# A graph layer on one core: the last 24 edge blocks in half steps, paced dense work, and a last layer with nodes as rows

## The chip, the cores and the metric

The kernel runs on one core of one Trainium2 chip. The metric is device time in microseconds (us) of one execution; "before" is the kernel as it stood, "after" the kernel with the change described below. The time of an execution is a little longer than the span of its trace, which runs from the first to the last instruction that the profiler recorded.

The engines are named as in the profile: PE is TensorE (matrix products; PEld its weight loads), DVE is VectorE (elementwise work), ACT is ScalarE (activations), POOL is GpSimd (here it only issues gathers), SP is SyncE (here it only issues the other transfers). A name with a q, as SPq, is an engine's sequencer.

## The reference

There are 8192 nodes with 256 channels and 131072 edges with 64 channels, sorted by destination. One graph layer with attention is computed, added to its input, and normalized:

```python
ea  = edge_attr @ w_e + b_e
msg = relu(x[src] + ea)
agg = segment_sum(msg, dst)                          # per destination node
h_local = bn(relu((x + agg) @ w1 + b1) @ w2 + b2 + x)
# attention inside groups of 32 nodes, 4 heads of 64 channels
h_attn  = bn(softmax(q k^T / 8) v @ out_w.T + out_b + x)
out = h_local + h_attn
out = bn3(out + relu(out @ m_w1 + m_b1) @ m_w2 + m_b2)
return layernorm(x + out)                            # over the 256 channels
```

Each `bn` is a multiplication and an addition by constants of the channel. All data are float32.

## The kernel before, in words

**Edges.** The edges are cut into NB = 128 blocks of 1024. For a block, `gather` (L152) has POOL issue eight indirect transfers, each of 128 rows of `x` (of `xb`, which is x + b_e, from block 20 on) into the tile `xs`, of which there are four. `load_edges` and `edge_transpose` bring the edge attributes and turn them. `edge_products` (L195) has PE multiply them by `w_e` into two double banks of PSUM, one for each pair of the block's four groups of 256 edges (tag `pe`, two buffers). `edge_messages` (L219) adds the gathered rows on DVE (L229) and takes the relu on ACT (L233). `edge_sums` (L255) multiplies the messages by one-hot matrices (L250, 16 PE instructions into the one bank with tag `pw`) and ACT copies the result to `ws` (L263). `edge_place` (L270) multiplies `ws` by a second one-hot matrix, which puts the rows at their nodes (L278, four PE instructions), and DVE adds that to the transposed node features `xT` (L287).

**Nodes.** The nodes are cut into 16 chunks of 512. `attention_front` and `attention_back` leave the attention's part in the tile `hA`, with channels as rows and nodes as columns. `dense` (L533) does the rest for a part of a chunk once all edge blocks that can reach its nodes are placed: layer w1 (ACT relu, L553), layer w2 (DVE adds it to `hA`, L556), layer m_w1 (ACT relu, L562), ACT's scaled copy `zT` of `hA` (L567), layer m_w2 (DVE adds it, scaled by s3, to `zT`, L574), PE transposes of `zT` back to nodes as rows (L583), the addition of x (L589), the normalization (L591 to L601), and the transfer out on SP's queue (L606). A layer's product for 128 nodes and 128 output channels is four PE instructions of 128 columns; it goes into one of three banks with tag `at`. The 128 nodes of the last quarter of chunk 15 need edge block 127, those of its third quarter block 126, of its second block 124, of its first block 122.

**Order.** PE's instructions are issued in the order in which the code emits them. DVE's and ACT's order is that of the code for the first 26 blocks; after that a scheduler sets it, and `tc.issue_after(i)` makes what follows stand behind instruction `i` on that engine. From block TAIL = 104 on, a plan written out by hand sets the order: a clock `t` is moved forward by an assumed cost for each step; rows of block i are assumed to have come at `came[i]` = 7.9 + 10.035 (i + 1); edge steps are emitted when they are due (`times`), and between them `Work.step` (L682) emits steps of four streams of node work in turns, at most one step of a stream each 0.5 us beyond its cost. `newest` holds the last `ws` copy and the last `xT` addition; the messages of a block are put behind both (L838 to L841). In the plan before, a block's products, messages and sums are emitted for the whole block at once, and block 127's messages are cut into pieces of one group and, for the last group, of 128 edges.

The last parts run in two streams, DENSE and DENSE2, with tiles of their own: chunk 14 in two halves, chunk 15 in four quarters. When the plan has placed block 127, `work.finish` emits what is left of both streams in turns.

Of the kernel before, what the change touches and what calls it, by code (L numbers as in the profile page):

```python
# [41 lines left out]
TAIL = 104  # L42
AGG_ROWS = N + 2 * P
# [29 lines left out]
def gnn_kernel(ctx: ExitStack, tc: tile.TileContext, x, src, dst, edge_attr, w, out):  # L73
# [62 lines left out]
    c3 = const.tile([P, KC], FP, name="c3")  # L136

# [55 lines left out]
    pe_of, msg_of, oh_of, newest = {}, {}, {}, {}  # L193
# [25 lines left out]
    def edge_messages(b):  # L219

        xs = xs_of.pop(b)
        msg = msg_of[b] = epool.tile([P, NH, TJ, C], FP, name="msg", tag="msg", bufs=3)
        n = 2 if b < NB - 1 else 1
        for h in range(0, NH, 2):
# [29 lines left out]

    def edge_sums(blocks):  # L255

        n = len(blocks)
        pw = pps.tile([P, 2, C], FP, name="pw", tag="pw", bufs=1)
        for i, b in enumerate(blocks):
            turns = [(h, j) for j in range(TJ) for h in range(NH)]  # L260
            group_sums(pw, i, b, sorted(turns) if b == NB - 1 else turns)
# [271 lines left out]
    def dense(n0, st, pool, bank, a=0, z=CH, own=("h1", "m1", "zT", "y", "")):  # L533
# [18 lines left out]
        for o in range(KC):  # L552
            nc.scalar.activation(h1[:, o, :], layer(w1, KC, o, tT), AF.Relu, bias=v_("b1", o))  # L553
            yield 1.7 * part
        for o in range(KC):
            nc.vector.scalar_tensor_tensor(  # L556
                hA[:, o, :], layer(w2, KC, o, h1), s1[:, o : o + 1], hA[:, o, :], op0=ALU.mult, op1=ALU.add
            )
            yield 1.7 * part
        m1 = pool.tile([P, 2 * KC, w], FP, name="m1", tag=own[1])  # L560
        for o in range(2 * KC):
            nc.scalar.activation(m1[:, o, :], layer(mw1, KC, o, hA), AF.Relu, bias=v_("m_b1", o))  # L562
            yield 1.7 * part
# [9 lines left out]
        for o in range(KC):  # L573
            nc.vector.scalar_tensor_tensor(  # L574
                zT[:, o, :], layer(mw2, 2 * KC, o, m1), s3[:, o : o + 1], zT[:, o, :], op0=ALU.mult, op1=ALU.add
            )
            yield 3.4 * part
# [26 lines left out]
        for wt, ts in groups:  # L604
# [3 lines left out]
            )  # L608
        yield 0.0
# [33 lines left out]
    class Work:  # L643
# [5 lines left out]
        def __init__(self, n):  # L649
            self.streams = [[] for _ in range(n)]  # L650
            self.rest, self.turn, self.owed = [0] * n, 0, 0.0
            self.at, self.placed_at = [0.0] * n, 0.0

# [28 lines left out]
        def step(self, t, until):  # L682

            n = len(self.streams)
            for i in [k % n for k in range(self.turn, self.turn + n)]:
                while self.streams[i] and self.streams[i][0][0]() and t >= self.at[i]:
# [6 lines left out]
                    elif d > 0:  # L693
                        t += d
                        self.at[i], self.turn = t + 0.5, (i + 1) % n
# [14 lines left out]
    with tc.manual_schedule(engines={PE}):  # L710
# [9 lines left out]
        for c in range(NCH):  # L720
# [11 lines left out]
            if c < NCH - 2:  # L732
                work.add(DENSE, summed(c), dense(c * CH, st, npool, bank))
        for i, c, a, z in (
            (DENSE2, NCH - 2, 0, CH // 2), (DENSE, NCH - 2, CH // 2, CH), (DENSE2, NCH - 1, 0, P),
            (DENSE, NCH - 1, P, 2 * P), (DENSE2, NCH - 1, 2 * P, 3 * P), (DENSE, NCH - 1, 3 * P, CH),
        ):
            d = dense(c * CH, chunk[c], npool, bank, a, z, *([OTHER] if i == DENSE2 else []))
# [10 lines left out]
        while b < TAIL:  # L749
# [11 lines left out]

            if b:
# [29 lines left out]
        t, p, m, s, l = came[b - 2] + 20, b, b, b - 2, b - 2  # L792
# [180 lines left out]
```

## Time and profile before

| | before |
|---|---|
| time, median of 3 runs | 1315.99 us (1314.24 to 1318.11) |
| profiled execution: time, span | 1315.85 us, 1314.1 us |
| PE, DVE, ACT, POOL busy | 91%, 61%, 45%, 74% of the span |
| mean granted TensorE clock | 0.96 |
| read from HBM, written to it | 222.06 MB, 16.78 MB |

In the page's groups a row gives the line, the engine, the operation, what it writes and reads, the count, then busy us and the mean ns of one, then the idle time just before them and what ended it. A row of the timeline gives the start and the duration in us, the engine, the line and the tiles of instructions merged into one row, and in brackets the idle time before it and what ended that. A row of the stretches gives, for a window in us, the length and mean of it, each engine's busy time with its count of instructions, the granted TensorE clock (1.00 is full), the share of DMA time and the GB/s. The profiler's matmul durations contain a pipeline latency, so the pace of matmuls is read from their starts.

### The profile page before, as it was taken

Reading aid. Unit: us, or ns where it says so; the run is one execution under the profiler, and the core shown is the slowest. Engines: PE = TensorE matmul, PEld = TensorE weight load, DVE = VectorE, ACT = ScalarE, POOL = GpSimd, SP = SyncE. Lnnn points to the kernel's source line nnn. Section 1 sums busy time; section 2 is a strip of 40 time slices with the busy share of each in tenths; the row PEclk is TensorE's granted clock in tenths of the full one; section 3 lists DMA queues with packets and bytes.
Section 4 is the critical chain, followed back from the end, with each engine's and each line's share of the span. In section 5 each row is a group of like instructions: output and inputs, shape, how many; then the busy total and the mean of one; then the engine's idle time right before and its main releaser. Section 6 shows DMA issues by size and latency. Waiting matters only on the chain.

```text
span 1314.1 us, 21073 instructions
## 1 busy us (share of the span) xinstructions
PE 1198.9 (91%) x7683; PEld 722.8 (55%) x7683; DVE 803.9 (61%) x1634; ACT 592.0 (45%) x850; POOL 975.3 (74%) x1032
## 2 busy tenths in 40 slices
PE   5987989999999989898997999889898999989986
PEld 3554646556565555555564555545555555555665
DVE  6567665757566565745746574565647558475663
ACT  2524444454545264443544444354454445453443
POOL 7777777777777777777777777777777777777772
PEclk8989999999999989898999999989899999999998
DMA  9999976677666666665767566576566567665741
GB/s 230 280 328 275 280 216 166 175 188 192 169 182 158 171 181 159 188 163 152 195 163 185 153 185 169 154 186 169 169 170 191 149 168 194 162 168 154 193 135 48
DMA packets 148922, 240.35 MB, mean 183 GB/s; under 512 B 27950, under 2 KB 112204, under 8 KB 148044
## 3 DMA queue, kind: packets, MB, share of 16 engines
q0 software_dynamic: 49152, 134.28, 38.6%
q1 hardware_dynamic: 98572, 104.65, 29.4%
q8 instruction: 62, 1.02, 0.3%
q14 instruction: 48, 0.39, 0.1%
q10 hardware_dynamic: 1088, 0.00, 0.0%
HBM read 222.06 MB, written 16.78 MB: 182 GB/s over the span
## 4 chain that ended last, share of the span: by engine, by line
POOL 34%; PE 31%; issue 16%; DMA 9%; DVE 8%; ACT 2%; SPq 0%; DVEq 0%; POOLq 0%; ACTq 0%
POOL xs L157 34%; PE at L546 8%; DMA xs<-xb,srci 6%; PE pe L208 6%; PE at L443 3%; PE pw L250 3%; PE pe L203 2%; PE at L524 2%; DVE msg L229 2%; PE l L278 1%; DVE bd L504 1%; PE at L512 1%; PE at L457 1%; DMA xb<-xp 1%; DVE eaT L190 1%
## 5 line engine op out<-in xcount | busy, mean ns | idle before, releaser
L157 POOL DMA_INDIRECT xs<-xb,srci x864 | 819.1, 948 | 263.2 <-issue 247.7
L233 ACT ACTIVATE msg<-msg 128x1024 f32<-128x1024 f32 (+1 forms) x259 | 270.0, 1046 | 401.4 <-DVE msg L229 397.4
L229 DVE TENSOR_TENSOR msg<-pe,xs 128x1024 f32<-128x1024 f32 (+1 forms) x259 | 306.6, 1207 | 196.5 <-PE pe L208 91.2
L208 PE MATMUL pe<-we,eaT 64*128 64x256 f32 x2048 | 270.3, 401 | 13.5 <-ACT pr L484 9.8
L208 PEld LDWEIGHTS pe<-we,eaT 64*128 64x128 f32 x2048 | 195.4, 194 | 117.9 <-issue 62.8
L157 POOL DMA_INDIRECT xs<-in_x_dram,srci x144 | 138.8, 964 | 43.9 <-issue 40.8
L250 PE MATMUL pw<-msg,oh 128*32 128x256 f32 x2048 | 129.8, 385 | 1.2 <-ACT msg L233 0.8
L546 PE MATMUL at<-hA,mw 128*128 128x512 f32 (+2 forms) x320 | 125.8, 520 | 4.5 <-DVE hA L556 4.3
L443 PE MATMUL at<-xT,inT 128*128 128x512 f32 x256 | 121.8, 602 | 3.2 <-ACT xT L433 3.2
L546 PE MATMUL at<-m,mw 128*128 128x512 f32 (+2 forms) x320 | 119.4, 517 | 0.0
L190 DVE STREAM_TRANSPOSE eaT<-ea 128x512 f32<-128x512 f32 x128 | 90.0, 703 | 22.0 <-PE pe L208 18.6
L250 PEld LDWEIGHTS pw<-msg,oh 128*32 128x32 f32 x2048 | 59.9, 110 | 63.6 <-issue 22.8
L278 PEld LDWEIGHTS l<-oh,ws 128*128 128x128 f32 x512 | 73.7, 195 | 27.3 <-issue 21.4
L278 PE MATMUL l<-oh,ws 128*128 128x160 f32 (+4 forms) x512 | 85.9, 308 | 1.8 <-ACT ws L263 1.7
L546 PEld LDWEIGHTS at<-hA,mw 128*128 128x128 f32 x320 | 55.1, 192 | 53.4 <-issue 41.2
L546 PEld LDWEIGHTS at<-m,mw 128*128 128x128 f32 x320 | 55.7, 192 | 48.0 <-issue 44.8
L443 PEld LDWEIGHTS at<-xT,inT 128*128 128x128 f32 x256 | 46.9, 191 | 57.4 <-issue 47.6
L446 ACT ACTIVATE qk<-at,vec 128x512 f32<-128x512 f32 x64 | 43.8, 685 | 73.7 <-PE at L443 73.6
L546 PE MATMUL at<-xT,w 128*128 128x512 f32 (+2 forms) x160 | 66.3, 551 | 8.8 <-DVE xT L287 8.8
L562 ACT ACTIVATE m<-at,vec 128x512 f32<-128x512 f32 (+2 forms) x80 | 47.9, 599 | 58.5 <-PE at L546 58.0
L546 PE MATMUL at<-h,w 128*128 128x512 f32 (+2 forms) x160 | 65.3, 532 | 9.4 <-ACT oT L519 7.0
L241 DVE TENSOR_TENSOR oh<-iota_n,rel 128x128 f32<-128x128 f32 x256 | 57.6, 279 | 18.2 <-PE pw L250 14.8
(111 smaller groups left out, 1200.7 us busy)
## 6 DMA issues: line engine op xcount, KB each, us to landing
ea<-in_edge_attr_dram SPq DMA_DIRECT2D x512, 128.0 KB
xs<-xb,srci POOLq DMA_INDIRECT x864
xn<-in_x_dram SPq DMA_DIRECT2D x16, 512.0 KB
out_dram<-y SPq DMA_DIRECT2D x14, 512.0 KB
xp<-in_x_dram SPq DMA_DIRECT2D x10, 512.0 KB
xb<-xp SPq DMA_DIRECT2D x10, 512.0 KB
xp<-in_x_dram SPq DMA_DIRECT2D x3, 1024.0 KB
xb<-xp SPq DMA_DIRECT2D x3, 1024.0 KB
```

Of the source, the lines that this page charges most:

```text
L157: nc.gpsimd.indirect_dma_start(out=xs[:, h, j, :], out_offset=None, in_=x if b < NX else xb[:, :], in_offset=bass.IndirectOffsetOnAxis(ap= ...
L190: nc.vector.transpose(eaT, ea[:, QR:].rearrange("p (g d) -> p g d", d=ED)[:, :, :QR])
L208: nc.tensor.matmul(pe[:, i, u, :], eaT[rows, h + u], we[rows, :], start=(b >= NX), stop=True, skip_group_check=True)
L229: nc.vector.tensor_add(msg[:, hs, js].rearrange("p u i c -> p i u c"), pe[:, js, u : u + n, :], xs[:, hs, js].rearrange("p u i c -> p i u c"),
L233: nc.scalar.activation(msg[:, hs, js], msg[:, hs, js], AF.Relu)
L241: nc.vector.tensor_tensor(oh[:, ts], iota_n[:, None, :WN].to_broadcast([P, TB // 2, WN]), rel[:, b, ts, None].to_broadcast([P, TB // 2, WN ...
L250: nc.tensor.matmul(pw[h * WN : (h + 1) * WN, i, :], oh_of[b][:, h * TJ + j, :], msg_of[b][:, h, j, :], start=(j == 0), stop=(j == TJ - 1), ...
L278: nc.tensor.matmul(l2[:, k, at : at + wn], ws[:, i, k * P : (k + 1) * P], oh2[:, i, :wn], start=(i == 0 and k == 0), stop=(i == last), ski ...
L443: nc.tensor.matmul(ps, inT[:, k, o * P : (o + 1) * P], xT[:, k, :], start=(k == 0), stop=(k == KC - 1))
L446: nc.scalar.activation(qk[:, o, :], ps, AF.Identity, bias=v_("in_b", o))
L546: nc.tensor.matmul(ps, wt[:, k, o * P : (o + 1) * P], act[:, k, :], start=(k == 0), stop=(k == nk - 1))
L562: nc.scalar.activation(m1[:, o, :], layer(mw1, KC, o, hA), AF.Relu, bias=v_("m_b1", o))
```

## The change

1. *Halves.* From block 104 on, products, messages and sums are emitted for two groups at a time (`pairs`, `some_sums`). The plan lets the first half's messages stand 2.5 us before the second half's. For block 127 the sums of three groups go first, and those of the last group after its rows. The gather of block i + 2 is emitted with the first half of block i's products. The messages now also stand behind the newest relu of node work on ACT and the newest addition of node work on DVE.
2. *Pacing.* Between `came[115]` and `came[124]` in the plan's clock, node work is given SHARE = 0.42 of the time. The second half of chunk 14 becomes two quarters.
3. *Rows.* `dense_rows` replaces `dense` for the quarters of chunk 15. The first three layers stay. The last one takes `m1` as the stationary and `mw2` as the moving operand, so that its result has nodes as rows; x + c3 (DVE, then a product with the identity), `hA` scaled by s3 (a product with a diagonal matrix) and the layer are summed in one bank, and normalized from there. Transposes, `zT` and its additions are gone for these parts. For the last quarter (`ahead`) the product of x + c3 is emitted before the sums of block 127's last group, and its banks come partly from the tag `pe`.
4. *Set-up.* At block 12 PE makes four transposes of s3 and c3; DVE multiplies `mw2` by s3, copies c3 as a row and makes the diagonal matrices. `dense` then adds with a plain addition instead of one with a scale.

```diff
-            nc.vector.scalar_tensor_tensor(
-                zT[:, o, :], layer(mw2, 2 * KC, o, m1), s3[:, o : o + 1], zT[:, o, :], op0=ALU.mult, op1=ALU.add
-            )
+            newest["dense"] = nc.vector.tensor_add(zT[:, o, :], layer(mw2, 2 * KC, o, m1), zT[:, o, :]).ins
...
+    def dense_rows(n0, st, pool, bank, a, own=("h1", "m1", "zT", "y", ""), ahead=False):
...
+        nc.vector.tensor_add(y, st["xn"][:, a // P, :], c3row)
+
+        def sum_of_x():
+            ps = bank()[:, :C]
+            nc.tensor.matmul(ps, ident, y, start=True, stop=False, skip_group_check=True)
+            return ps
...
+        if ahead:
+            out_ps = sum_of_x()
+            yield 0.45
+        h1 = pool.tile([P, KC, P], FP, name="h1", tag=own[0])
+        for o in range(KC):
+            for _, ps in layer(w1, KC, [o], xT):
+                newest["relu"] = nc.scalar.activation(h1[:, o, :], ps, AF.Relu, bias=v_("b1", o)).ins
+            yield 0.45
+        for o, ps in layer(w2, KC, range(KC), h1):
+            newest["dense"] = nc.vector.scalar_tensor_tensor(
+                hA[:, o, :], ps, s1[:, o : o + 1], hA[:, o, :], op0=ALU.mult, op1=ALU.add
+            ).ins
+        yield 0.9
+        m1 = pool.tile([P, 2 * KC, P], FP, name="m1", tag=own[1])
+        for o0 in range(0, 2 * KC, 2):
+            for o, ps in layer(mw1, KC, range(o0, o0 + 2), hA):
+                newest["relu"] = nc.scalar.activation(m1[:, o, :], ps, AF.Relu, bias=v_("m_b1", o)).ins
+            yield 0.9
+        if not ahead:
+            out_ps = sum_of_x()
+            yield 0.45
+        for k in range(KC):
+            nc.tensor.matmul(
+                out_ps[:, k * P : (k + 1) * P], hA[:, k, :], diag[:, k, :], start=False, stop=False,
+                skip_group_check=True,
+            )
+        yield 0.45
+        for k in range(2 * KC):
+            nc.tensor.matmul(
+                out_ps, m1[:, k, :], mw2[:, k, :], start=False, stop=(k == 2 * KC - 1), skip_group_check=True
+            )
+            if k == KC - 1:
+                yield 0.9
+        nc.vector.bn_stats(st6, out_ps)
+        nc.vector.bn_aggr(mv, st6)
+        nc.scalar.activation(rstd, mv[:, 1:2], AF.Sqrt, bias=eps_t)
+        yield 0.9
+        nc.vector.reciprocal(rstd, rstd)
+        nc.vector.tensor_scalar(y, out_ps, mv[:, 0:1], rstd, ALU.subtract, ALU.mult)
+        nc.sync.dma_start(out[ds(n0 + a, P), :], y)
...
+            if self.paced_from <= t < self.paced_to:
+                self.credit += SHARE * (t - max(self.seen, self.paced_from))
+                self.seen = t
+                if self.credit < -0.02:
+                    return min(until, t - self.credit / SHARE)
...
+            if b == 12:
+                ps = bank()[:, : 2 * C].rearrange("p (i c) -> p i c", i=2)
+                for i, cols in enumerate((s3, c3)):
+                    for k in range(KC):
+                        nc.tensor.transpose(
+                            ps[:, i, k * P : (k + 1) * P], cols[:, k : k + 1].to_broadcast([P, P]), ident
+                        )
+                nc.vector.tensor_mul(mw2, mw2, ps[:, 0, None, :].to_broadcast([P, 2 * KC, C]))
+                nc.vector.tensor_copy(c3row, ps[:, 1, :])
+                for k in range(KC):
+                    nc.vector.tensor_scalar(diag[:, k], ident, s3[:, k : k + 1], None, ALU.mult)
...
+        work.paced_from, work.paced_to = came[115], came[124]
...
-            if l < s:
-                times[0] = summed_at[l] + 1.5
-            elif s < m:
-                times[1] = max(added[s] + 1.2, bank_free)
-                if s == NB - 1:
-                    times[1] = max(came[s] + 2.2, bank_free)
-            if p < NB - 1 and m == p:
-                times[2] = added[p - 1]
-            if m < p:
-                times[3] = came[m]
+            if l < s[0]:
+                times[0] = summed_at[l] + 0.7
+            elif (s[0], s[1] + (s[0] == NB - 1)) < tuple(m):
+                i, k = s
+                times[1] = max(added[i, k] + 1.2, bank_free)
+                if i == NB - 1:
+                    times[1] = max(came[i] + (0.2, 1.0)[k], bank_free)
+            if p[0] < NB and (p[0] - 1, p[1]) < tuple(m):
+                times[2] = added[p[0] - 1, p[1]]
+            if tuple(m) < tuple(p):
+                times[3] = came[m[0]] - 2.5 * (1 - m[1])
...
+                some_sums(i, last if k else range(last.start))
+                t += 0.14 * TJ * (len(last) if k else last.start)
+                if k:
+                    sums = edge_sums([i])
+                    summed_at[i] = t
+                elif i == NB - 1:
+                    next(last_part)
```

More of the change, by code (lines that the diff above doesn't have):

```diff
@@ L253, in group_sums, with some_sums @@
             )
+    def some_sums(b, groups):
+        if b not in pw_of:
+            pw_of[b] = pps.tile([P, 2, C], FP, name="pw", tag="pw", bufs=1)
+        group_sums(pw_of[b], 0, b, [(h, j) for h in groups for j in range(TJ)])
     def edge_sums(blocks):
         n = len(blocks)
[L258 to L261, printed above, removed]
+        pw = pw_of.pop(blocks[0], None)
+        if pw is None:
+            pw = pps.tile([P, 2, C], FP, name="pw", tag="pw", bufs=1)
+            for i, b in enumerate(blocks):
+                group_sums(pw, i, b, [(h, j) for j in range(TJ) for h in range(NH)])
         ws = epool.tile([P, 2, C], FP, name="ws", tag="ws", bufs=2)
```

117 lines of the change are left out of this document (78 added, 39 removed).

## The prediction

> **What bounds the kernel now.** I read the page first, then POOL's rows of the timeline, then the timeline of the last 50 us with all engines, and the granted clock there.
>
> ```profile
> span 1314.1 us, 21073 instructions
> PE 1198.9 (91%) x7683; PEld 722.8 (55%) x7683; DVE 803.9 (61%) x1634; ACT 592.0 (45%) x850; POOL 975.3 (74%) x1032
> ...
> L157 POOL DMA_INDIRECT xs<-xb,srci x864 | 819.1, 948 | 263.2 <-issue 247.7
> ```
>
> ```profile
> 4.31 1.10 POOL L157 DMA_INDIRECT xs<-in_x_dram,srcd  x1 [2.71 <-issue]
> ...
> 1288.01 0.95 POOL L157 DMA_INDIRECT xs<-xb,srci  x1 [0.30 <-issue]
> 1289.26 0.94 POOL L157 DMA_INDIRECT xs<-xb,srci  x1 [0.30 <-issue]
> ```
>
> PE is the busiest engine, but POOL sets the pace: its 74% is a gather of 0.95 us, then 0.30 us of issue, without a wait. 1023 steps of 1.25 us (1289.26 - 1288.01) make 1279 of the 1284.95 us between the first gather and the last. So nothing ahead of 1289.26 moves the end unless it stops a gather. What a change can win is the tail behind it:
>
> ```profile
> 1276.33 1.07 PE L250 MATMUL pw<-msg,oh 128*32 128x256 f32 x16
> ...
> 1279.25 0.94 POOL L157 DMA_INDIRECT xs<-xb,srci  x1 [0.30 <-issue]
> ...
> 1282.08 1.23 DVE L229 TENSOR_TENSOR msg<-pe,xs 128x1024 f32<-128x1024 f32 x1 [1.34 <-DMA xs<-xb,srci]
> ...
> 1283.34 1.06 ACT L233 ACTIVATE msg<-msg 128x1024 f32<-128x1024 f32 x1 [1.77 <-DVE msg L229]
> ...
> 1283.62 0.47 PE L583 MATMUL at<-ident,zT 128*128 128x128 f32 x1 [2.29 <-DVE zT L574]
> ...
> 1284.03 2.35 PE L250 MATMUL pw<-msg,oh 128*32 128x256 f32 x16
> ...
> 1288.32 1.17 PE L278 MATMUL l<-oh,ws 128*128 128x96 f32 x4
> ...
> 1289.80 1.28 DVE L229 TENSOR_TENSOR msg<-pe,xs 128x512 f32<-128x512 f32 x2
> ...
> 1291.17 1.35 DVE L229 TENSOR_TENSOR msg<-pe,xs 128x512 f32<-128x512 f32 x3
> ...
> 1291.89 0.62 ACT L233 ACTIVATE msg<-msg 128x512 f32<-128x512 f32 x1
> ...
> 1292.67 0.71 ACT L233 ACTIVATE msg<-msg 128x256 f32<-128x256 f32 x2
> ...
> 1294.62 1.09 PE L250 MATMUL pw<-msg,oh 128*32 128x256 f32 x16
> ...
> 1295.86 0.37 ACT L263 COPY ws<-pw 128x256 f32<-128x256 f32 x1 [0.77 <-PE pw L250]
> ...
> 1296.29 0.69 PE L278 MATMUL l<-oh,ws 128*128 128x96 f32 x4 [0.57 <-ACT ws L263]
> ...
> 1297.39 0.71 PE L546 MATMUL at<-xT,w 128*128 128x128 f32 x4 [0.42 <-DVE xT L287]
> 1297.83 0.53 PEld L546 LDWEIGHTS at<-hA,mw 128*128 128x128 f32 x4
> ...
> 1298.14 0.37 ACT L553 ACTIVATE h<-at,vec 128x128 f32<-128x128 f32 x1 [1.90 <-PE at L546]
> 1298.27 0.53 PEld L546 LDWEIGHTS at<-xT,w 128*128 128x128 f32 x4
> ...
> 1300.87 0.35 DVE L556 SCALAR_TENSOR_TENSOR hA<-at,s,hA 128x128 f32<-128x128 f32 x1 [0.54 <-PE at L546]
> ...
> 1307.91 0.43 DVE L591 BATCH_NORM_STATS2 st<-y 128x6 f32<-128x256 f32 x1
> ...
> 1309.56 0.33 SPq L606 DMA_DIRECT2D out_dram<-y  x1
> ```
>
> ```profile
> 1279.89:1283.30 3.41, 1.44 (x13) 1.20 (x11) 2.07 (x4) 1.06 (x1) 2.50 (x4) 1.00 0.31 96
> 1283.30:1290.13 6.83, 6.51 (x33) 3.68 (x35) 2.90 (x10) 1.72 (x3) 5.31 (x6) 0.50 0.49 132
> 1290.13:1296.95 6.82, 5.88 (x48) 3.93 (x44) 3.09 (x8) 4.55 (x11) 0.07 (x1) 1.00 0.09 25
> ```
>
> Four things are to be seen. A gather's rows are there 2.83 us after its start (1279.25 to 1282.08), so the last come at 1289.26 + 2.83 = 1292.09, inside DVE's row at 1291.17. PE stood idle 2.29 us behind an addition (zT) that DVE had put behind a message waiting for rows, and then ran 6.83 us at a clock of 0.50: 16 sums took 2.35 us, not 1.07. Block 127's sums began at 1294.62, 1.24 us after its last relu (1292.67 + 0.71), because PE had node work queued ahead. And from its placement (1296.29) to the last transfer out (1309.56) the chain takes 13.27 us, with the third quarter's layers interleaved on PE. Then 4.5 us to the end of the span, and 1.75 us outside it.
>
> **The change, part by part.**
>
> *Gathers.* The halves, the pacing and the new order on POOL's queue move no gather: each finds its `xs` buffer free, and the plan emits it no later than before. That cover could end at one place only, the set-up at block 12, where the messages run far behind their rows:
>
> ```profile
> 173.11 2.90 PE L512 MATMUL at<-bd,vn 128*64 128x128 f32 x32 [2.18 <-DVE bd L504]
> ...
> 182.31 1.23 DVE L229 TENSOR_TENSOR msg<-pe,xs 128x1024 f32<-128x1024 f32 x1 [1.18 <-PE pe L208]
> ...
> 184.03 1.22 DVE L229 TENSOR_TENSOR msg<-pe,xs 128x1024 f32<-128x1024 f32 x1 [0.50 <-PE pe L208]
> ...
> 188.10 0.94 POOL L157 DMA_INDIRECT xs<-in_x_dram,srci  x1 [0.30 <-issue]
> ```
>
> These are the messages of block 14, done at 185.25, and the gather of block 18, which takes over their buffer 2.85 us later. The set-up puts on DVE a product of 128x1024 from PSUM (1.23, as a message), a copy of 128x256 (about 0.4, a third of that) and two small ones (about 0.25 each): 2.1 us. DVE's delay reaches PE at 173.11, where PE waits for DVE, and so block 14: 2.85 - 2.1 leaves 0.75 us, and no gather stops. The bounds are 0 and +0.9 us (set-up at 3.7 us, with the four transposes on top); I take 0.
>
> *Up to block 127's placement.* The plan's arithmetic (its costs, due times and turns, followed through for both versions) gives this order on PE behind block 126's second half of sums: the third quarter needs w1, w1, w2 and its m_w1 pairs, then the sums of three groups of block 127, the x product of the last quarter, the sums of group four, the x product of the third quarter, placement. I follow it at full clock. Block 126's rows come at 1282.08 as before; relu done 1284.40 (1283.34 + 1.06); eight sums 0.53 (half of 1.07); two blocks of m1 with `mw2` for the second quarter, four instructions of 256 columns:
>
> ```profile
> 1061.03 1.73 PE at L457 x8
> ```
>
> at 0.216 each 0.86 us; placement at 1285.9, not 1288.32. From a placement to the first w1 it is 1.10 us (1296.29 to 1297.39), plus 0.3 for the second quarter's statistics on DVE: 1287.3. A group of four instructions takes 0.44 us (PEld rows 1297.83, 1298.27) and its result is read 0.75 us after its start (1297.39 to 1298.14). So w1 twice, relu, second half of w2, two additions: 1287.3 + 0.44 + 0.75 + 0.37 + 0.44 + 0.31 + 0.55 = 1290.15. Here the change adds a wait: block 127's messages now stand behind these additions on DVE. Its five pieces (1.28 + 1.35) end at 1292.8, 0.3 later than before. Then ACT is the limit: the last relus stand behind the four relus of the third quarter's m_w1 (4 x 0.37), with five message relus (3 x 0.62 + 0.71) 4.05 us from about 1290.9, that is 1294.95. Group four's four sums, copy and placement take 1.67 us (1294.62 to 1296.29) less twelve sums (0.80): placement at 1295.8. With 0.2 us of waits between: 1296.0, against 1296.29. **-0.3 us.** Scheduler and PE's queue are not shown by any row: if ACT took the message relus first, placement would be at about 1294.0 (-2.3); if PE is late by one such idle time as 2.29, +2. I take the middle, which follows the emitted order.
>
> *From the placement to the last transfer out.* In time from the last quarter's first w1: w1 0 to 0.44, third quarter's diagonal to 0.89, w1 to 1.34, third quarter's last layer to 2.20, w2 to 3.09, its rest to 3.95, m_w1 to 5.73 (hidden: relus, additions), diagonal (four instructions) to 6.18, last layer (eight at 0.216) to 7.91. Statistics read the bank 0.35 us later, and from there to the transfer is 1.65 us (1307.91 to 1309.56), at the same durations though the source is PSUM. With the 1.10 us ahead: 11.0 us instead of 13.27. **-2.3 us.** What goes: both zT additions, the transposes, the x addition, and 12 of the third quarter's m_w1 instructions, now ahead of the placement; what comes, diagonal and x products, lies beside other work or costs 0.44. Bounds: a PSUM-read statistics at twice 0.43 and a bank wait of 0.5 give -1.3; all of the third quarter out of the way gives -3.5. The 4.5 us behind stays: same 128 KB.
>
> *At no cost.* Pacing from 1172 to 1262 on the plan's clock moves work that PE does beside the gathers; if that cover is gone PE is late in the stage above (its +2). A plain addition instead of one with a scale is at most as long.
>
> Sum: -0.3 - 2.3 = -2.6; 1315.85 - 2.6 = **1313.2 us**. The profiled 1315.85 stands 0.14 under the median of 1315.99, so this is -0.2%: a gain too small for the bound of 0.3% (3.95 us: 1312.04 to 1319.94), about what a measurement of this kernel can tell from no change.
>
> **Rivals.**
>
> *A, the halves win in full.* DVE's and ACT's order favour block 127: placement 2.3 us earlier, rest 2.3 us: 1315.85 - 4.6 = 1311.2. For it: the rows are there at 1292.09, 4.2 us ahead of the old placement. Against: the change itself puts these messages behind more work.
>
> *B, the clock falls in the new tail.* PE waits about 1.5 us for ACT before group three's sums. Before, a stretch of 3.41 us with 1.44 us busy was followed by 6.83 us at 0.50; there the extra cost was 1.28 on sums and 0.48 on a placement (1288.32 against 1296.29). 6.83 us at half clock lose 3.4 us of matmul, and 7.9 of the 11.0 us behind the placement are matmul, so 2.4 of it are lost: 1315.6. The Trainium skill (TensorE: Matmul & The Clock Gate, section on why this matters for your kernels) warns only of PE gaps over about 3 us; by that the clock would hold here, but the trace shows it falling after 2.29 us, so the row decides and B keeps its chance.
>
> *C, slower: the clock stays at 0.50 from 1283 to the end.* On the path above 7.9 us of matmul behind the placement and 1.6 ahead of it (sums 0.53 and 0.27, two placements at 0.4) would double: 1313.2 + 9.5 = 1322.7. It decides from 6.7 us of doubled work on (1319.94), which takes two such stretches and more. Against: every stretch after 1290.13 was at 1.00.
>
> *D, it does not do what it says.* PE is late at 1284 by the waits seen before, and loses the 2.3 us again: 1315.6.
>
> **How the numbers follow.** Forecast 0.32, A 0.27, B 0.17, D 0.13, C 0.11. The forecast's own range is 1312.1 to 1314.8. Over the cases the range reaches from 1310.4 (A with more of its bound) to 1317.4 (B with 2 us of PE's lateness), leaving out C and a little below. Faster by over 0.3%: A and a little of the forecast, 0.29; within: 0.58; slower: C and the end of B, 0.13.
>
> **What would show it.** Right: gathers still 1.25 us apart up to about 1289.3 with the one of block 18 unmoved; block 126's placement near 1286; block 127's near 1296 with ACT busy from 1291 to 1295; 11 us from there to the last transfer; clock 1.00 from 1283 on. Wrong: a gather waiting near 188, the placement at 1294 (A), a clock of 0.50 behind 1290 (B, C), or a PE idle of over 1 us between 1277 and 1285 (D).

## The result, and the profile after

The kernel after takes 1354.79 us (median of 4 runs, 1354.19 to 1355.17) against 1316.01 us before (4 runs): a ratio of 1.0294, with a 95% interval of 1.0276 to 1.0311. The change makes the kernel 38.8 us slower. The prediction was 1313.2 us, with a range of 1310.4 to 1317.4. In many of the sessions behind the experiments below, the kernel before itself took 1963 to 2026 us and PE was busy only some 70 % of the span, so that a cost on PE shows there only in part; every ratio is to runs of before on the same chip in the same session.

From the page of the kernel after (its profiled execution took 1355.02 us):

```profile
span 1353.2 us, 21140 instructions
PE 1231.5 (91%) x7719; PEld 734.6 (54%) x7719; DVE 801.6 (59%) x1636; ACT 591.2 (44%) x851; POOL 977.5 (72%) x1032
```

PE is busy 32.6 us longer than before (1198.9) with 36 instructions more; the busy times of DVE, ACT and POOL change by less than 3 us. Where PE's time went is seen in the groups of its instructions from 1080 us to the end (busy us, mean ns, idle before). After:

```profile
L255 PE MATMUL pw<-msg,oh 128*32 128x256 f32 x360 | 51.9, 402 | 2.8 <-ACT msg L238 2.8
L211 PE MATMUL pe<-we,eaT 64*128 64x256 f32 x338 | 49.7, 415 | 10.7 <-DVE msg L234 8.6 <-ACT pr L496 2.1
```

Before:

```profile
L208 PE MATMUL pe<-we,eaT 64*128 64x256 f32 x352 | 46.3, 400 | 4.2 <-DVE msg L229 2.7 <-ACT pr L484 1.5
L250 PE MATMUL pw<-msg,oh 128*32 128x256 f32 x368 | 27.6, 396 | 1.2 <-ACT msg L233 0.8 <-DVE xT L287 0.4
```

The mean of one sum is the same (402 and 396 ns), and yet the group's busy time goes from 27.6 to 51.9 us. The timeline of PE after shows how:

```profile
1143.14 1.06 PE L255 MATMUL pw<-msg,oh 128*32 128x256 f32 x8
1144.14 1.14 PE L211 MATMUL pe<-we,eaT 64*128 64x256 f32 x8
1145.20 1.06 PE L255 MATMUL pw<-msg,oh 128*32 128x256 f32 x8
...
1336.11 1.05 PE L255 MATMUL pw<-msg,oh 128*32 128x256 f32 x4
```

Eight sums of a half block take 1.06 us. Sixteen sums of a whole block took 1.07 us (the row at 1276.33 in the prediction), and the last group alone, four sums, takes 1.05 us. The four column groups of `pw` run side by side, four instructions at a time: of block 127's sums before, four start within 0.04 us of 1294.62 and no other by 1294.80. A half block has two groups, so it has as many steps with half the instructions in each. A block's sums now cost PE 2.1 us.

The two kernels in the same stretch, 1072 to 1300 us (columns: length, then busy us and instructions of PE, PEld, DVE, ACT, POOL, then granted clock, DMA share, GB/s). Before, then after:

```profile
1072.00:1300.00 228.00, 209.73 (x1411) 132.41 (x1407) 143.91 (x306) 103.58 (x171) 165.18 (x175) 0.99 0.60 159
```

```profile
1072.00:1300.00 228.00, 207.95 (x1210) 118.78 (x1208) 127.13 (x268) 89.82 (x143) 165.12 (x174) 0.97 0.59 157
```

PE is as busy as before, but has 201 instructions fewer behind it at 1300 us. That debt shows in two places. First, messages fall so far behind that gathers wait for their buffers. POOL's rows after, three of them with idle time, and the last gather:

```profile
1187.54 0.94 POOL L160 DMA_INDIRECT xs<-xb,srci  x1 [5.24 <-DVE oh L279]
...
1210.24 0.95 POOL L160 DMA_INDIRECT xs<-xb,srci  x1 [2.85 <-DVE msg L234]
...
1232.75 0.95 POOL L160 DMA_INDIRECT xs<-xb,srci  x1 [2.75 <-DVE msg L234]
...
1302.02 0.95 POOL L160 DMA_INDIRECT xs<-xb,srci  x1 [0.30 <-issue]
```

The last gather starts 12.76 us later than before (1289.26). The three waits make 9.9 us of this (their idle time less the usual 0.30 us each). The rest is a gather of 949 ns instead of 946 in the median, over the whole kernel; it does not come from the halves, as 1.8 us of it are there at block 104's first gather (1051.86 against 1050.08). Second, the rest of PE's work stands behind it. From the last gather's end to block 127's placement, after and before:

```profile
1302.93:1337.63 34.70, 32.95 (x221) 22.43 (x220) 16.82 (x42) 12.13 (x29) 0.04 (x1) 1.00 0.05 16
```

```profile
1290.20:1296.29 6.09, 5.15 (x45) 3.34 (x41) 3.02 (x8) 4.55 (x11) 0.00 (x0) 1.00 0.09 27
```

34.70 us instead of 6.09, with PE busy for 32.95 of them: PE is the bound here, not the rows. The end, after:

```profile
1337.63 0.68 PE L290 MATMUL l<-oh,ws 128*128 128x96 f32 x4
...
1347.02 0.43 DVE L679 BATCH_NORM_STATS2 st<-pe 128x6 f32<-128x256 f32 x1 [2.27 <-PE pe L674]
...
1348.80 0.33 SPq L685 DMA_DIRECT2D out_dram<-y  x1
```

From the placement to the last transfer it is 11.17 us (before 13.27). The sum: 12.76 for the gathers, 28.61 for PE's queue (34.70 - 6.09), less 2.10 for the shorter end, is 39.3 us, against 39.1 us between the spans.

### The profile page after: what moved, and what is told of

It reads as the page before. It is cut to its first block, busy times and chain, and to the rows that moved or that the text cites. A ratio compares the mean times of both kernels' runs of the same rounds, so it can differ in the third digit from the quotient of the medians.

```text
span 1353.2 us, 21140 instructions
## 1 busy us (share of the span) xinstructions
PE 1231.5 (91%) x7719; PEld 734.6 (54%) x7719; DVE 801.6 (59%) x1636; ACT 591.2 (44%) x851; POOL 977.5 (72%) x1032
## 4 chain that ended last, share of the span: by engine, by line
PE 41%; POOL 25%; issue 13%; DMA 9%; DVE 8%; ACT 3%; DVEq 0%; SPq 0%; POOLq 0%; ACTq 0%
POOL xs L160 25%; PE at L558 11%; PE pe L211 8%; DMA xs<-xb,srci 5%; PE pw L255 4%; PE at L455 4%; PE at L536 3%; DVE msg L234 2%; PE l L290 2%; PE pe L206 2%; PE at L469 2%; PE at L524 1%; DVE bd L516 1%; DMA ea<-in_edge_attr_dram 1%; PE at L641 1%
## 5 line engine op out<-in xcount | busy, mean ns | idle before, releaser
L211 PE MATMUL pe<-we,eaT 64*128 64x256 f32 x2048 | 272.6, 399 | 20.7 <-DVE msg L234 10.4
L211 PEld LDWEIGHTS pe<-we,eaT 64*128 64x128 f32 x2048 | 191.8, 192 | 133.2 <-issue 65.8
L255 PE MATMUL pw<-msg,oh 128*32 128x256 f32 x2048 | 154.9, 386 | 2.8 <-ACT msg L238 2.8
L558 PE MATMUL at<-hA,mw 128*128 128x512 f32 (+2 forms) x272 | 118.8, 560 | 2.7 <-DVE hA L568 2.5
L558 PE MATMUL at<-m,mw 128*128 128x512 f32 (+2 forms) x272 | 111.5, 553 | 0.0
L255 PEld LDWEIGHTS pw<-msg,oh 128*32 128x32 f32 x2048 | 68.6, 110 | 74.2 <-issue 25.7
L558 PEld LDWEIGHTS at<-hA,mw 128*128 128x128 f32 x272 | 47.8, 192 | 51.7 <-issue 43.1
L558 PEld LDWEIGHTS at<-m,mw 128*128 128x128 f32 x272 | 48.8, 192 | 48.4 <-issue 46.3
L558 PE MATMUL at<-h,w 128*128 128x512 f32 (+2 forms) x136 | 61.8, 577 | 8.5 <-ACT oT L531 7.1
L574 ACT ACTIVATE m<-at,vec 128x512 f32<-128x512 f32 (+2 forms) x68 | 43.2, 635 | 56.7 <-PE at L558 56.7
L586 DVE TENSOR_TENSOR zT<-at,zT 128x512 f32<-128x512 f32 (+2 forms) x34 | 21.3, 626 | 76.8 <-PE at L558 76.7
L246 DVE TENSOR_TENSOR oh<-iota_n,rel 128x128 f32<-128x128 f32 x256 | 57.6, 278 | 13.7 <-PE pw L255 13.7
```

Source lines behind the costliest of these rows:

```text
L211: nc.tensor.matmul(pe[:, i, u, :], eaT[rows, h + u], we[rows, :], start=(b >= NX), stop=True, skip_group_check=True)
L246: nc.vector.tensor_tensor(oh[:, ts], iota_n[:, None, :WN].to_broadcast([P, TB // 2, WN]), rel[:, b, ts, None].to_broadcast([P, TB // 2, WN ...
L255: nc.tensor.matmul(pw[h * WN : (h + 1) * WN, i, :], oh_of[b][:, h * TJ + j, :], msg_of[b][:, h, j, :], start=(j == 0), stop=(j == TJ - 1), ...
L558: nc.tensor.matmul(ps, wt[:, k, o * P : (o + 1) * P], act[:, k, :], start=(k == 0), stop=(k == nk - 1))
L574: newest["relu"] = nc.scalar.activation(m1[:, o, :], layer(mw1, KC, o, hA), AF.Relu, bias=v_("m_b1", o)).ins
```

## The experiments

Three theories stood at the start. S: half a block's sums cost PE as much as a whole block's. P: the pacing leaves too much node work for the end. W: messages wait on DVE and ACT because they now stand behind the newest relu and addition of the node layers. A fourth, H (the halves of products and messages), was added when S had explained only part.

The runs beside a kernel before of about 2000 us stand in a table of their own behind the others.

**The sums whole again** (rest of the change as it is):

```
 def some_sums(b, groups):
...
-    group_sums(pw_of[b], 0, b, [(h, j) for h in groups for j in range(TJ)])
+    if b < NB - 1:
+        groups = range(NH) if groups.stop == NH else range(0)
+    group_sums(pw_of[b], 0, b, [(h, j) for j in range(TJ) for h in groups])
```

The edit also changes the order of the sums, from group by group to one step of all groups after another. That is no rival: before, block 127's sixteen sums stand group by group and take 1.09 us (the row at 1294.62 in the prediction).

> All of the change, but the sums of blocks 104 to 126 whole; once more, for a chip that runs the kernel before in some 1316 us. Theory S (half a block's sums take PE as long as a whole block's): PE's busy time 22 to 26 us below 1231.5, no gather waits from 1150 on, time 1313 to 1322 us. Theory P (pacing): 1340 us or more. Theory W (messages behind node work): 1335 us or more.

Measured: 1338.82 us against 1319.18, ratio 1.0155 (1.0124 to 1.0186). Its page, its waits of PE (us in total, times, longest) and the same stretch as above:

```profile
span 1337.8 us, 21134 instructions
PE 1208.3 (90%) x7719; PEld 725.2 (54%) x7719; DVE 802.1 (60%) x1636; ACT 591.1 (44%) x851; POOL 975.3 (73%) x1032
...
L255 PE MATMUL pw<-msg,oh 128*32 128x256 f32 x2048 | 129.2, 383 | 1.6 <-ACT msg L238 1.6
```

```profile
PE pe L211 <- DVE msg L234: 13.7, 13, 4.1
```

```profile
1072.00:1300.00 228.00, 200.21 (x1304) 121.12 (x1300) 135.26 (x285) 93.32 (x153) 165.36 (x175) 0.98 0.60 160
```

Two of S's three marks came out in the main. PE's busy time falls by 23.2 us. The gathers' long waits go: the longest idle times left are 0.94 and 0.80 us, and the last gather starts 1.35 us later than before, not 12.76:

```profile
1290.61 0.95 POOL L160 DMA_INDIRECT xs<-xb,srci  x1 [0.30 <-issue]
```

The third did not: the time falls by 1.4 % (1.0294 to 1.0155, some 18 us), not by 2.9 %. The time lies in the range named for W (1335 us or more) and 1 us below the one for P. In the stretch PE now is idle 27.8 us (228.00 - 200.21) where before it was idle 18.3, and it waits 13.7 us for messages ahead of products (before 2.7 us, the group of L208 above). So the half sums are one cause, and 20 us, nearly all of them behind the last gather, have another.

**Messages not behind node work, sums whole**: W's part taken away too.

```
-                    for i in newest.values():
-                        behind.enter_context(tc.issue_after(i))
+                    for key in ("ws", "xT"):
+                        behind.enter_context(tc.issue_after(newest[key]))
```

> The kernel after with two parts undone: the sums of blocks 104 to 126 whole, and messages put behind the newest copy of sums and the newest placement alone. Halves of products and messages, pacing and the last layer with nodes as rows stay. With the sums whole alone 1338.8 us were measured (before 1319.2), 16 of the 39 us; PE then waited 13.7 us for messages ahead of products between 1072 and 1300, where before it waited 2.7. Theory W (messages stand behind node work on DVE and ACT, so PE waits for the banks they free): that wait falls below 6 us and the time is 1316 to 1326 us. Theory H (a half block's product on PE follows the half message that frees its banks, whatever the message stands behind): the wait stays over 10 us, time 1332 to 1342 us. Theory P (pacing): the same, 1332 to 1342 us.

Measured: 1334.81 us against 1316.57, ratio 1.0135 (1.0106 to 1.0165). PE still waits 9.7 us for messages ahead of products: less than 13.7, but not the 6 or less that W asked for. W said 1316 to 1326 us and is refuted as the main cause; the time lies in the range that H and P shared, and H's wait of over 10 us is just missed. Whether W is worth the 0.2 % between the two ratios, these intervals don't tell.

**No pacing either**: sums whole, messages as before, and

```
-        work.paced_from, work.paced_to = came[115], came[124]
+        work.paced_from, work.paced_to = 1e9, 0.0
```

> The kernel after with three parts undone: sums whole, messages behind the sums' copy and the placement alone, no pacing. What is left of the change is the halves of products and messages with the new order and costs of the plan, the third quarter in a piece of its own, and the last layer with nodes as rows. With pacing still in, 1334.8 us were measured (before 1316.6). Theory P (pacing holds node work back until it stands behind the last gather): 1314 to 1322 us. Theory H (the halves of products and messages make PE wait for banks, 9.7 us between 1072 and 1300 with 4.1 us at 1103.6, and cost 0.1 us a product): 1328 to 1337 us, with the same idle time near 1103.

> The same kernel once more (sums whole, messages behind the sums' copy and the placement alone, no pacing), for a chip that runs the kernel before in some 1316 us. Theory P (pacing): 1314 to 1322 us. Theory H (halves of products and messages): 1328 to 1337 us, with idle time of PE near 1103 as before.

Measured (the first of the two stands in the table below): 1342.70 us against 1316.77, ratio 1.0194 (1.0152 to 1.0236). P said 1314 to 1322 us and is refuted: without pacing the kernel is no faster. It is 0.6 % slower than with it, but the intervals overlap (1.0165 against 1.0152), so that the pacing is worth anything is not shown. H's range (1328 to 1337) was missed by 5.7 us; the idle time near 1103 that it named is there (4.14 us, below). What is left of the change here, beside the last layer with nodes as rows, is the halves of products and messages with the plan's new costs and due times, and the second half of chunk 14 in two quarters.

**The last layer with nodes as rows alone**: the loop over the last 24 blocks as before (sums, products and messages whole, no pacing), the four parts of the last chunk by `dense_rows`, and the set-up at block 12.

```
-            d = dense(c * CH, chunk[c], npool, bank, a, z, *([OTHER] if i == DENSE2 else []))
+            if c < NCH - 1:
+                d = dense(c * CH, chunk[c], npool, bank, a, z, *own)
+            elif z < CH:
+                d = dense_rows(c * CH, chunk[c], npool, bank, a, *own)
+            else:
+                d = last_part = dense_rows(c * CH, chunk[c], npool, lambda: next(last_banks), a, ahead=True)
...
+                if s == NB - 1:
+                    next(last_part)
                 sums = edge_sums([s])
```

> The kernel before with one part of the change alone: the four parts of the last chunk have the last layer with nodes as rows, summed in one bank with x and hA, and the set-up of this at block 12 (scaled weights, one row, diagonals). No halves, no pacing, messages behind the sums' copy and the placement alone, the order of the last 24 blocks as before. All theories agree on the stretch ahead of the last placement (as before); from there to the last transfer the prediction said 11.0 us for 13.27, so 1312 to 1315 us where before takes 1316. If the set-up stops a gather near block 18, or the pieces of the new tail wait for each other, 1316 us or more.

Measured: 1316.60 us against 1316.45, ratio 0.9999 (0.9983 to 1.0015; 8 runs): no change. From its timeline:

```profile
1290.34 0.94 POOL L160 DMA_INDIRECT xs<-xb,srci  x1 [0.30 <-issue]
...
1295.42 0.60 PE L635 MATMUL pe<-y,ident 128*128 128x256 f32 x2
1295.95 1.09 PE L255 MATMUL pw<-msg,oh 128*32 128x256 f32 x16
1297.61 0.69 PE L291 MATMUL l<-oh,ws 128*128 128x96 f32 x4 [0.57 <-ACT ws L276]
...
1309.82 0.54 DVE L685 TENSOR_SCALAR y<-pe,mv,rstd 128x256 f32<-128x256 f32 x1
```

From the placement to the end of the last DVE instruction it is 12.75 us, of 13.27 before to the transfer: 0.5 us gained, not 2.1. Here half of the third quarter's m_w1, its diagonal and its last layer still stand behind the placement on PE; in the kernel after the order had put the m_w1 ahead of it. The placement itself is 1.32 us later (1296.29 before), 1.08 of it from the gathers (1289.26 before).

This run and the one without pacing differ by the halves of products and messages, by the plan that goes with them (due times, costs, block 127's sums in two steps) and by the second half of chunk 14 in two quarters: 0.9999 against 1.0194. So H, taken with its plan and these two quarters, holds some 1.9 %, 25 us, without pacing; the quarters were not tried apart. Where PE loses it is seen from one placement to another with about as much node work between (blocks 104 to 119). Each time the stretch, and then the group of products in it; with rows alone:

```profile
1072.40:1220.40 148.00, 140.47 (x874) 80.54 (x874) 95.61 (x200) 66.28 (x102) 112.06 (x119) 0.98 0.64 167
```

```profile
L211 PE MATMUL pe<-we,eaT 64*128 64x256 f32 x224 | 28.9, 395 | 3.2 <-DVE msg L234 1.6 <-ACT pr L497 1.5
```

With halves:

```profile
1071.30:1237.80 166.50, 150.91 (x889) 83.66 (x889) 96.90 (x204) 68.20 (x103) 124.27 (x132) 0.95 0.63 165
```

```profile
L211 PE MATMUL pe<-we,eaT 64*128 64x256 f32 x232 | 34.9, 429 | 10.0 <-DVE msg L234 7.6 <-ACT pr L498 2.4
```

18.5 us more: 10.4 busy and 8.1 idle. 6.8 of the idle time are waits ahead of products. Of the busy time some 5 us are the clock, by an estimate from the two stretches: 166.50 us at 0.95 are 8.3 us short of full speed, 148.00 us at 0.98 only 3.0. The products' own 6.0 us are of three kinds: eight instructions more (1.1 us); three halves behind a wait that take 2.07 to 2.08 us at half clock, not 1.13 (2.8 us, where with rows alone one block behind a wait loses 0.7); and at full clock two halves that take 2.27 us where a whole block takes 2.00. So the waits, with the low clock that follows them, are the larger part (some 13 of the 18.5 us), and the halves' products themselves the smaller. The largest of these waits, in the run with halves (PE, then DVE):

```profile
1097.77 1.88 PE L560 MATMUL at<-xT,w 128*128 128x512 f32 x4
1103.79 2.08 PE L211 MATMUL pe<-we,eaT 64*128 64x256 f32 x8 [4.14 <-DVE msg L234]
1105.80 3.78 PE L560 MATMUL at<-xT,w 128*128 128x512 f32 x4
```

```profile
1099.84 1.27 DVE L601 TENSOR_TENSOR y<-at,xn 128x512 f32<-128x512 f32 x2
...
1102.55 1.19 DVE L234 TENSOR_TENSOR msg<-pe,xs 128x1024 f32<-128x1024 f32 x1
```

PE's next product needs the bank that the half message at 1102.55 frees, and this message stands on DVE behind a chunk's normalisation. PE runs its list in order, so the eight products hold up all node work behind them. With products whole the same place has this row:

```profile
1098.58 2.68 PE L211 MATMUL pe<-we,eaT 64*128 64x256 f32 x16 [1.64 <-DVE msg L234]
```

A wait of 1.64 us, not 4.14. That the half product comes to stand earlier in PE's list than a whole one did is what the plan's due times say (due as soon as the same half of the block before has its message); it was not tried apart from the new costs in the plan, so which of the two makes most of the 25 us stays open.

**Half sums alone on the kernel before** (`first_sums` emits groups 0 and 1 at the time of the old sums, the rest 0.3 us later, other work of PE between):

```
+            elif t >= times[1] and s not in pw_of and s < NB - 1:
+                first_sums(s)
+                t += 0.6
+                second_at = t + 0.3
```

> The kernel before with only its sums of blocks 104 to 126 in halves, for a chip that runs the kernel before in some 1316 us. If half sums cost time by themselves (1.0 us of PE a block, 23 us, against some 20 us of idle time of PE between 1072 and 1300): 1322 to 1340 us. If they hurt only on top of the halves of products and messages: 1314 to 1320 us.

All six runs of this kernel stand beside a kernel before of 1967 to 2026 us, so this is not settled by them. Their rows show the mechanism:

```profile
1718.04 1.06 PE L250 MATMUL pw<-msg,oh 128*32 128x256 f32 x8 [1.45 <-DVE mv L603]
1720.95 1.06 PE L250 MATMUL pw<-msg,oh 128*32 128x256 f32 x8
```

and all six ratios are above 1 (0.3 to 1.8 %), three of them with their whole interval.

**The runs beside a kernel before of about 2000 us.** The same kernels, and with them two more edits of the kernel after, each by itself: the pacing out, and the messages not behind node work, as in the diffs above. What was expected stands here by kernel, each time for a kernel before of 1316 us. Sums whole:

> The kernel after, but the sums of blocks 104 to 126 are emitted whole, as before: sixteen instructions at the second half's turn, none at the first's. Everything else of the change stays. Theory S (eight instructions of a half block use two of four column groups and take 1.06 us, as sixteen did, so each block costs PE some 1.0 us more, 23 to 24 us over the 23 blocks, in a stretch where PE has hardly any idle time): the busy time of PE falls by 22 to 26 us, the gathers' waits of 6.18, 3.8 and 3.7 us go, and the time is 1313 to 1322 us. Theory P (pacing leaves too much node work for the end): the sums' time comes free, but the node work is still held back; the time stays at 1340 us or more. Theory W (messages wait on DVE and ACT behind the newest node work): gathers still wait near 1187, time 1335 us or more.

> The same kernel as in the run with whole sums before (all of the change, but the sums of blocks 104 to 126 whole), to be had on a chip on which the kernel before takes some 1316 us, since on the first chip it took 2011.75 us, with engines idle for their next instruction, and PE busy only 69 % of the span, so that 24 us of PE's time had nowhere to show. Theory S: PE's busy time 22 to 26 us below that of the kernel after (1231.5), no gather waits from 1150 on, time 1313 to 1322 us. Theory P: 1340 us or more. Theory W: 1335 us or more.

> All of the change, but the sums of blocks 104 to 126 whole; third time, now that a chip ran the kernel before in 1316 us. Theory S (half a block's sums take PE as long as a whole block's): PE's busy time 22 to 26 us below 1231.5, no gather waits from 1150 on, time 1313 to 1322 us. Theory P (pacing leaves too much node work for the end): 1340 us or more. Theory W (messages wait behind the newest node work on DVE and ACT): 1335 us or more.

Before with half sums:

> The kernel before, with one thing of the change: the sums of blocks 104 to 126 in two halves of eight instructions, with other work of PE between them. No pacing, messages whole, no layer with nodes as rows. Theory S: PE's busy time rises by 22 to 26 us, its messages fall behind their rows, and the time is 1330 to 1345 us. Theories P and W: 1314 to 1319 us, as before.

> The kernel before with the sums of blocks 104 to 126 in two halves, once more, to be had where the kernel before takes some 1316 us. Theory S: PE's busy time 22 to 26 us above that of before (1198.9), messages behind their rows from block 106 on, time 1330 to 1345 us. Theories P and W: 1314 to 1319 us.

> The kernel before with one thing of the change: the sums of blocks 104 to 126 in two halves of eight instructions. Theory S: PE's busy time 22 to 26 us above 1198.9, time 1330 to 1345 us. Theories P and W: 1314 to 1319 us.

> The kernel before with one thing of the change: the sums of blocks 104 to 126 in two halves of eight instructions, other work of PE between them; products and messages whole, no pacing. By what the runs show so far: half sums cost PE 1.0 us a block, 23 us over 23 blocks; before, PE had some 20 us of idle time between 1072 and 1300, so the sums alone should make 1322 to 1340 us. If the half sums hurt only together with the halves of products and messages, 1314 to 1320 us.

> The kernel before with only its sums of blocks 104 to 126 in halves, a last time, for a chip that runs the kernel before in some 1316 us. If half sums cost time by themselves: 1322 to 1340 us. If they hurt only on top of the halves of products and messages: 1314 to 1320 us.

No pacing alone:

> The kernel after without the pacing of node work from block 115 to block 124; all else of the change stays. Theory P: the node work held back goes back beside the gathers, the tail behind the last gather shortens from some 50 us towards 24, and the time is 1316 to 1325 us. Theory S: PE has no room beside the gathers either, so the gathers only wait more and the tail is shorter by as much; the time is 1345 to 1358 us.

> The kernel after without the pacing from block 115 to block 124. Theory P: 1316 to 1325 us. Theory S: PE has no room beside the gathers either; 1345 to 1358 us.

Messages not behind node work alone:

> The kernel after, but a block's messages are put behind the newest copy of sums and the newest placement alone, as before, and not behind the newest relu and the newest addition of the node layers too. Theory W: the messages are taken up as their rows come, the gathers at 1187, 1210 and 1233 us do not wait, and the time is 1316 to 1325 us. Theory S: what makes the messages late is PE's products and sums, not the order on DVE and ACT; the time is 1345 to 1358 us.

> The kernel after with a block's messages put behind the newest copy of sums and the newest placement alone, as before. Theory W: the gathers near 1187, 1210 and 1233 us do not wait; 1316 to 1325 us. Theory S: 1345 to 1358 us.

| kernel | before, us | ratio (95 % interval) |
| --- | --- | --- |
| sums whole | 2011.75 / 1966.51 / 1968.21 | 1.0270 (1.0197-1.0344) / 1.0154 (1.0100-1.0209) / 1.0157 (1.0026-1.0288) |
| before with half sums | 2011.75 / 2019.86 / 1968.21 | 1.0177 (1.0108-1.0246) / 1.0182 (1.0114-1.0250) / 1.0061 (1.0024-1.0099) |
| the same, later runs (the second is the one expected above) | 2026.49 / 2023.12 / 1967.41 | 1.0044 (0.9996-1.0093) / 1.0033 (0.9954-1.0111) / 1.0171 (0.9931-1.0410) |
| no pacing | 2011.75 / 1968.21 | 2059.32 us, one run / 1.0141 (1.0031-1.0250) |
| messages not behind | 2011.75 / 1968.21 | 2046.07 us, one run / 1.0186 (1.0008-1.0364) |
| sums whole, not behind, no pacing | 1962.77 | 1.0066 (1.0028-1.0105) |

None of these tells S, P and W apart: gathers wait for messages all through the kernel (613 us in all in one run with sums whole, 2.7 us in the kernel before at 1315.85), and the ratio of one and the same kernel moves from session to session by as much as the kernels differ (1.0154 to 1.0270 with sums whole, 1.0033 to 1.0182 for before with half sums). They agree with the others in this much: no kernel with any part of the halves was faster than before by its median, and undoing one part alone brought none of them back to 1.00.

## Why the prediction was wrong, point by point

**The step that failed first** is "eight sums 0.53 (half of 1.07)". Eight take 1.06 us, and four (the last group, taken as 0.27, twelve being 0.80) take 1.05. The prediction used the figure only for block 126 and block 127, as 0.5 us on the path, and did not ask what the same term does to the 23 blocks ahead of them. There it is 23 x 1.05 = 24 us of PE (24.3 in the groups of L255 and L250, 23.2 when the sums were whole again), in a stretch in which PE had 18.3 us idle. Undone, it gives 18 of the 39 us by the ratios (16 by the two times, which are of different sessions). The row for the right price stood in the trace of before: at the prediction's own 0.216 us for an instruction of 256 columns, sixteen one after another would take some 3.5 us; in 1.07 us they can only have run side by side, and the form 128*32 says that each uses 32 of the columns. The Trainium skill has the rule (TensorE: Matmul & The Clock Gate, Part 3 on packing small matmuls): tiles at different positions run at the same time, and a pack lasts as long as one matmul plus about 4 ns for each further tile. By it two groups cost what four do; the rows here agree, with 1.06 and 1.07 us.

**The second step that failed** is "The halves, the pacing and the new order on POOL's queue move no gather", and with it halves that stand in the sum at no price. The cover named was that each gather finds its buffer free. It was checked at one place, block 12, and held there. In the last 24 blocks what hid PE's work was PE's own idle time beside the gathers, and the halves took more than that: 24 us by the sums, and by the halves of products and messages waits for banks (7.6 us between blocks 104 and 119, 1.6 with rows alone), some 5 us of lower clock, and 0.27 us for each whole block's products cut in two at full clock. I named a price only for PE being late by one idle time (+2); the runs show 20 us of lateness from this part even with the sums whole. How much of it is the halves and how much the new due times stays open.

**Block 12** was right: the set-up stops no gather. Block 14's second message ends at 185.00, and block 18's gather starts 3.27 us later (2.85 before). The kernel after:

```profile
183.77 1.23 DVE L234 TENSOR_TENSOR msg<-pe,xs 128x1024 f32<-128x1024 f32 x1 [0.50 <-PE pe L211]
...
188.27 0.94 POOL L160 DMA_INDIRECT xs<-in_x_dram,srci  x1 [0.31 <-issue]
```

**"Up to block 127's placement", -0.3 us**, was wrong because its start was: the placement came at 1337.63, not 1296.0, with PE and not ACT behind it. The sums' price was wrong on this path too: from the last group's first sum to the placement it is 1.52 us (1336.11 to 1337.63), where the sum has 1.67 less 0.80.

**"From the placement to the last transfer", 11.0 us**, measured 11.17: right for the kernel after, and in its steps too: the statistics start 8.29 us after the first w1 (1338.73 to 1347.02), 8.26 in the sum. Only, with rows alone it is 12.75, so the gain of 2.1 us belongs to the plan's order with the third quarter's m_w1 ahead of the placement. In the kernel after, this order delays nothing: PE was some 29 us late with everything, and block 127's rows had come long before PE reached its sums. Whether it pays with PE on time no run shows. No run shows the layer with nodes as rows to be worth anything by itself (0.9999).

**The pacing** shows no cost, as said: without it (with sums whole) the time is 0.6 % longer, at intervals that overlap, so a gain by it is not shown either.

**The rivals.** C named slower, by the clock; the clock was 1.00 from 1302.93 to the placement and 1.00 from there to the last transfer, so it fell with B. D came nearest: PE late by its waits, but at +2 us. No rival had PE itself as the bound over the last 24 blocks, though the first thing read was that PE was busy 91 % of the span. The answer "POOL sets the pace" was true for the kernel before, with some 8 % of slack on PE (18.3 of 228.00 us), and the half sums alone asked for 24 us. Neither the rivals nor the range had a case for it.

**A version that beats both** was not found: the best variant, rows alone, equals the kernel before within 0.2 %.

## What to carry to other kernels

Before a piece of work is cut in two, look at whether its instructions run side by side: sixteen in 1.07 us and eight in 1.06 us cost the engine the same per piece, so two halves cost double. Where one engine sets the pace and another is 92 % busy beside it, price every edit on the second one for the whole stretch, as instructions times blocks against its idle time there, and not only on the path at the end. A finer pipeline on an engine that runs its list in order can also bring its waits forward: here a half piece that waits 4 us for a bank holds up everything listed behind it.

## What the runs showed of the hardware

One, two, three and four groups of four sums take 1.05, 1.06, 1.06 and 1.07 us (the twelve of three groups at 1320.56 in the run with whole sums and no pacing).

PE's clock after a wait. In the run with whole sums and no pacing, behind the idle time of 4.14 us that ended at 1103.79 (columns as above):

```profile
1096.60:1103.40 6.80, 3.05 (x16) 1.74 (x14) 6.71 (x16) 0.69 (x1) 5.28 (x6) 1.00 0.63 144
1103.40:1110.20 6.80, 6.41 (x16) 2.97 (x18) 3.71 (x11) 4.17 (x5) 4.97 (x7) 0.50 0.87 253
```

6.8 us at 0.50 follow, in which eight products take 2.08 us instead of 1.14: the wait costs about 3 us of matmul on top of its own 4. The Trainium skill (TensorE: Matmul & The Clock Gate, section on how the clock's oscillation bites in real kernels) puts the limit at a gap of about 3.4 us; this wait agrees, while the 2.29 us in the prediction fell short of it and was followed by 0.50 as well. The same holds for the 1.64 us at 1098.58 in the run with rows alone: PE was busy 1.76 us of the 3.40 from 1096.80, and the 3.40 us behind them ran at 0.51. Here the measurements decide: a wait of half that length can be enough.
